# Strassen's products for pairs of q, k and v chunks in an attention and large-kernel convolution block

## The chip, the cores and the metric

The kernel runs on one core of a Trainium2 chip. The metric is the device time of one launch in microseconds (us); three runs of the kernel before gave 2863.83, 2867.12 and 2868.03 us, median 2867.12. A profiled execution is taken besides, and every reading of the trace is of that one.

The engines are named as in the profile: PE is TensorE (PEld its weight loads), DVE is VectorE, ACT is ScalarE, POOL is GpSimd, SP is SyncE, which here only issues DMAs. SBUF is the memory from which they work, PSUM the small memory into which TensorE writes its products.

## The reference

```python
x = x + attn(group_norm(x))            # x: 1 x 384 x 192 x 192, float32
x = x + convs(group_norm(x))
...
def attn(x):
    qkv = einsum('bchw,oc->bohw', x, w_qkv) + b_qkv      # 3*384 outputs, 384 inputs
    qkv = qkv.reshape(b, 3 * c, 96, 2, 96, 2).max(axis=(3, 5))
    qkv = depthwise_conv_3x3(qkv, w_dw) + b_dw
    q, k, v = split(qkv, 3, axis=1)                      # 8 heads of 48 channels
    q, k = q / norm(q), k / norm(k)                      # over the 9216 places
    attn = einsum('bhcn,bhdn->bhcd', q, k) * temperature
    out = sum(a_i * topk_softmax(attn, k_i) @ v)         # k_i = 24, 32, 36, 38
    return w_proj @ repeat_2x2(gelu(out)) + b_proj
...
def convs(x):   # seven depthwise convolutions of sizes 13 to 3, each with its own scale and shift, summed
```

Inputs, outputs and all arithmetic are float32.

## The kernel before

The 384 channels are three chunks of 128 partitions, so q, k and v together have nine output chunks, m = 0 to 8 (q: 0 to 2, k: 3 to 5, v: 6 to 8).

**Statistics (lines 289 to 585).** The whole of x is read once for the group statistics. Some q, k products of the first six blocks are made meanwhile: for the keys in `EARLY` (blocks 0 to 5, chunks 0 to 2, first sub-block) the two first input chunks are multiplied (line 429, `multiply`), ACT copies the half-made result to SBUF (`put_by`, line 440), and later back to PSUM (`fill`, line 269), where only the third input chunk is added.

**The stage that changes (lines 992 to 1051).** x is read again, twice, in 24 blocks of 8 rows, each of two sub-blocks of 4 rows (`sb`). The first pass (B = 0 to 23) makes q and k, the second (B = 24 to 47) v. A step is one output chunk of one sub-block: `project` (line 671) makes six products of 128x128 weights with 128x384 columns (three input chunks times two row pairs) into one PSUM tile of two banks; two such tiles take turns. `pool` (lines 683 and 690) takes the maximum over each 2x2 cell with one DVE reduction of 768 columns, and ACT adds the bias and writes 128x192 into the padded map `pool_t`. Once both sub-blocks of a chunk are there, `begin` (line 703, ACT) writes the centre tap of the depthwise 3x3 convolution, `taps` (line 719, DVE) adds the other eight, four to a step, each one instruction over 128x384, and `end` squares q and k for their norms (line 733) and moves the two last rows to the top of the padded map for the next block (line 738). After the last q, k chunk of a block, `turn` transposes the results in three pieces (TensorE line 748, ACT line 750) and `add_gram` adds them to the gram matrix (line 760). In the second pass the softmax of the gram matrix runs in small steps (`attend`, lines 797 to 945), one call a step.

The order on each engine is the order in which the program emits instructions, in this stage and in the one after: the list `late` (lines 949 to 952) says after how many steps each piece is emitted. Beside this, ACT normalizes x in place (line 651, six a block), POOL adds 2x2 cells of x for later (`sum_up`, lines 280 to 284), ACT and POOL spread the convolution's filters into DRAM (`strip`, lines 779 and 788), and SP's queue loads x two blocks deep (line 179).

**After it.** Attention times v (line 1131) needs, from its seventh block on, a copy that DVE makes of one head's rows (line 1102), behind two statistics of stored sums for each earlier block (line 1088). Then come the output projection (line 1459) and the large convolution (line 1371), which the change leaves alone.

## Time and profile before

| what | us |
|---|---|
| median of three runs | 2867.12 |
| the profiled execution | 2862.88 |
| its span | 2861.1 |
| PE busy, whole span | 2735.6 (96%) |
| DVE busy | 2498.5 (87%) |
| ACT busy | 1332.9 (47%) |
| POOL busy | 917.3 (32%) |
| first pass of the stage that changes | 166.3 to 1333.2 |
| second pass | 1333.2 to 1904.6 |
| attention times v, from its first product to the projection's | 1905.7 to 1960.8 |

The profile's slices cut the span in 40 equal parts of 71.5 us; a digit is the busy share in tenths. A group line gives line, engine, operation, the output and inputs by the program's names, the shape, the count, the busy time in us, the mean ns of one instruction, and the idle time of the engine just before the group's instructions with what ended it. Mean duration and rate differ: TensorE starts a product instruction every 0.323 us though one takes 486 ns from start to end. The granted TensorE clock was 0.995 of full speed.

### The profile page before, as it was taken

To read this page: it belongs to the slowest core of one execution; us is meant where nothing else is said; L and a number is where in the kernel's file an instruction comes from. 1 tells how busy PE (TensorE), PEld (TensorE's weight loads), DVE (VectorE), ACT (ScalarE), POOL (GpSimd) and SP (SyncE) were. 2 spreads that over 40 slices of the span, in tenths; PEclk is the share of its full clock that TensorE was granted. 3 is DMA by queue.
4 is the path that set the end of the run, shared out by engine and by line. 5 is a ranking of instruction groups with operands and counts; after the bars stand their busy time and mean duration, and the time that the engine had idled before them with its cause. 6 is when DMAs were issued, how large, how long until landed. Compare 5 with 4: busy or idle time off the path is not lost.

```text
span 2861.1 us, 37738 instructions
## 1 busy us (share of the span) xinstructions
PE 2735.6 (96%) x13662; PEld 1677.2 (59%) x13662; DVE 2498.5 (87%) x3484; ACT 1332.9 (47%) x2427; POOL 917.3 (32%) x1129
## 2 busy tenths in 40 slices
PE   0699999999999999999999999999999999999998
PEld 0356666666666666666655555545566666666666
DVE  6879998888878888788899998888789999999997
ACT  3755554444444444454444444444334444444443
POOL 4251231332323223241222222232114445444443
PEclk9899999999999999999999999999999999999999
DMA  9942432232422324232333333328889999999996
GB/s 389 419 151 65 134 114 87 81 126 72 135 74 92 111 70 137 67 126 81 100 108 107 108 109 116 115 69 234 234 206 282 270 275 275 256 271 271 270 275 168
DMA packets 269561, 475.75 MB, mean 166 GB/s; under 512 B 25858, under 2 KB 189968, under 8 KB 269248
## 3 DMA queue, kind: packets, MB, share of 16 engines
q1 hardware_dynamic: 204208, 301.51, 38.2%
q0 software_dynamic: 43328, 149.04, 15.5%
q10 hardware_dynamic: 21840, 22.81, 2.3%
q8 instruction: 108, 1.77, 0.3%
q14 instruction: 77, 0.63, 0.1%
HBM read 337.06 MB, written 136.20 MB: 165 GB/s over the span
## 4 chain that ended last, share of the span: by engine, by line
PE 85%; DVE 7%; DMA 5%; ACT 1%; issue 1%; POOL 0%; ACTq 0%; SPq 0%; DVEq 0%; POOLq 0%
PE qkv L671 51%; PE conv L1371 24%; PE pj L1459 4%; DVE v L719 3%; DMA xs<-in_x 3%; PE gram L760 2%; PE tr L748 2%; PE av L1131 1%; DVE mx L683 1%; PE qkv L429 1%; DVE acc L719 1%; DVE stats L535 1%; DMA v<-in_x 0%; DMA smj<-sums 0%; DMA wt<-zd 0%
## 5 line engine op out<-in xcount | busy, mean ns | idle before, releaser
L671 PE MATMUL qkv<-xt,wqk 128*128 128x384 f32 x3304 | 1082.5, 486 | 1.9 <-DVE mx L683 1.1
L671 PEld LDWEIGHTS qkv<-xt,wqk 128*128 128x128 f32 x3304 | 620.1, 190 | 417.1 <-DVE mx L683 4.5
L719 DVE SCALAR_TENSOR_TENSOR acc<-pooled,wd,acc 128x384 f32<-128x384 f32 (+2 forms) x1152 | 733.7, 637 | 30.6
L1371 PE MATMUL conv<-xp,wt 128*64 128x288 f32 (+1 forms) x6016 | 723.9, 404 | 2.4 <-issue 1.7
L690 ACT ACTIVATE pooled<-mx,bq 128x192 f32<-128x192 f32 x432 | 196.8, 456 | 900.2 <-DVE mx L683 898.1
L1371 PEld LDWEIGHTS conv<-xp,wt 128*64 128x64 f32 x6016 | 462.9, 137 | 260.8 <-issue 2.7
L683 DVE TENSOR_REDUCE mx<-qkv 128x192 f32<-128x768 f32 x432 | 412.3, 954 | 200.1 <-PE qkv L671 187.1
L671 PE MATMUL qkv<-xt,wv 128*128 128x384 f32 x1728 | 562.4, 487 | 2.5 <-DVE mx L683 2.2
L671 PEld LDWEIGHTS qkv<-xt,wv 128*128 128x128 f32 x1728 | 326.0, 190 | 233.4 <-DVE mx L683 9.8
L1351 DVE STREAM_TRANSPOSE xp<-xn 128x4608 f32<-128x4608 f32 (+1 forms) x107 | 445.4, 4163 | 18.0 <-PE conv L1371 10.6
L280 POOL TENSOR_TENSOR sum<-xt 128x192 f32<-128x192 f32 x128 | 87.9, 687 | 969.0 <-ACT xt L651 968.0
L719 DVE SCALAR_TENSOR_TENSOR v<-pooled,wd,v 128x384 f32<-128x384 f32 (+2 forms) x576 | 375.4, 652 | 15.2
L1379 ACT ACTIVATE co<-conv,cb 128x288 f32<-128x288 f32 x376 | 186.9, 497 | 386.1 <-PE conv L1371 381.3
L651 ACT ACTIVATE xt<-xt,gn 128x768 f32<-128x768 f32 x278 | 275.5, 1014 | 0.0
L1328 POOL TENSOR_TENSOR raw<-raw,up 128x2496 f32<-128x2496 f32 x46 | 230.0, 5001 | 38.2 <-DMA up<-pd 27.6
L1421 POOL DMA_DIRECT2D out<-o x194 | 107.4, 582 | 373.5 <-DVE o L1412 315.2
L1412 DVE STREAM_TRANSPOSE o<-co 128x2304 f32<-128x2304 f32 (+3 forms) x50 | 211.0, 4222 | 9.6 <-ACT co L1403 8.8
L1459 PE MATMUL pj<-v,wp 128*128 128x384 f32 x432 | 142.6, 489 | 1.0 <-ACT v L1138 0.7
L788 POOL DMA_DIRECT2D zd<-v x96 | 72.0, 756 | 216.1 <-ACT v L779 216.1
L1336 ACT ACTIVATE xn<-raw,par 128x2112 f32<-128x2112 f32 x48 | 103.1, 2148 | 25.4 <-POOL raw L1328 21.8
L1459 PEld LDWEIGHTS pj<-v,wp 128*128 128x128 f32 x432 | 80.9, 190 | 55.9 <-ACT v L1138 1.4
L281 POOL TENSOR_TENSOR sum<-sum,xt 128x192 f32<-128x192 f32 x128 | 100.9, 789 | 10.8
(296 smaller groups left out, 1914.6 us busy)
## 6 DMA issues: line engine op xcount, KB each, us to landing
xt<-in_x SPq DMA_DIRECT2D x96, 1152.0 KB, 7.4
raw<-in_x SPq DMA_DIRECT2D x182, 312.0 KB, 13.2
out<-o POOLq DMA_DIRECT2D x188, 288.0 KB, 8.4
wt<-zd SPq DMA_DIRECT2D x46, 1024.0 KB, 12.2
zd<-v POOLq DMA_DIRECT2D x96, 416.0 KB, 4.4
up<-pd SPq DMA_DIRECT2D x184, 156.0 KB, 12.6
xs<-in_x POOLq DMA_DIRECT2D x20, 768.0 KB, 10.7
smj<-sums SPq DMA_DIRECT2D x72, 192.0 KB, 3.0
```

The lines of the kernel that those rows point to most:

```text
L651: nc.scalar.activation(xt[:, j], xt[:, j], AF.Identity, bias=gn0[:, j, 1:2], scale=gn0[:, j, 0:1])
L671: nc.tensor.matmul(ps[:, r, : 2 * W], lhsT=wq[:, j, mm * P : (mm + 1) * P], rhs=xt[:, j, r * 2 * W : (r + 1) * 2 * W], start=(j == 0), sto ...
L683: nc.vector.tensor_reduce(mx, ps[:, :, : 2 * W].rearrange("p r (y w x) -> p r w y x", y=2, x=2), AX.XY, ALU.max,)
L690: nc.scalar.activation(pool_t[m][:, k : k + SR, 1 : 1 + WS], mx, AF.Identity, bias=bq[:, m : m + 1])
L719: nc.vector.scalar_tensor_tensor(acc[:, :nt], pool_t[m][:, k0 + dy : k0 + dy + nt, dx : dx + WS], wd[:, m, t : t + 1], acc[:, :nt], ALU.mu ...
L1328: eng.tensor_add(rv, rv, uv.unsqueeze(2).to_broadcast([P, (m1 - m0) * WS, 2]))
L1351: nc.vector.transpose(bass.AP(at.tensor, at.offset, [list(at.ap[0]), [NBQ, n], [1, NBQ], [NQ * NBQ, CC], [ME * NBQ, NE]],), bass.AP(row.te ...
L1371: nc.tensor.matmul(ps[h * MH : (h + 1) * MH, t0:t1], lhsT=wt[:, c, o : o + MH], rhs=d[:, c, g + 2 * t0 : g + 2 * t1 - 1 : 2, :], start=(e ...
L1379: nc.scalar.activation(co[:, c], ps, AF.Identity, bias=cb[:, cc : cc + 1])
L1412: nc.vector.transpose(bass.AP(at.tensor, at.offset, [list(at.ap[0]), [2 * W, n], [BC, NBQ], [W, 2], [1, BC]]), bass.AP(of.tensor, of.offse ...
L1421: engines[u % len(engines)].dma_start(out=bass.AP(out.tensor, out.offset + k * CC * HW + (2 * u + t0 * BR) * W, [[ME * UQ * W, CC * NE], [ ...
L1459: nc.tensor.matmul(ps, lhsT=wp[:, j, i * P : (i + 1) * P], rhs=v[:, j, b * RB : (b + 1) * RB, :].rearrange("p r w -> p (r w)"), start=(j = ...
```

## The change

**Seven products for eight.** Two output chunks form a pair: (3,4), (0,1), (2,5) and, for v, (6,7); chunk 8 stays single. The operands of Strassen's form are the pair's weights for input chunks 0 and 1, and the even and odd rows (y = 0, 1) of the sub-block in these chunks. `mix` forms four sums of weights (POOL, once for each pair), `differ` four differences of x for each sub-block (POOL, 128x384 each) and stores them in DRAM; the second pass reads them back (`differ_again`, SP's queue) and doesn't form them again. Input chunk 2 is multiplied as before. A product is now 128x128 with 128x384 columns of one row parity, that is two runs of 192 columns.

**Seeds.** Each PSUM bank is a tile of its own (six `banks`, where there were two tiles of two banks each). Partial sums that serve two results are copied from bank to bank by ACT (`seed`), and TensorE adds further products to both. A finished even-row result is copied to SBUF by ACT (`moved`), DVE takes the maximum with the odd-row result from PSUM (`larger`), one more DVE addition closes the second chunk of the pair, and `pool` takes the maximum of neighbours. The bias is no longer added here: it is folded into the convolution's bias (`shifted`), and the padding holds its negative (`pad`).

**Early results.** Half-made results are copied from and to PSUM in two instructions of 384 columns instead of one of 768 (`put_by`, `fill`); in the stage `put` takes the place of `fill`. The statistics' own small products use two of the six banks.

**Taps of v over two blocks.** `begin` and the taps of v run over 8 rows (768 columns) once in two blocks; block 0 (3 rows) and block 23 (5 rows) stay apart. `carry` copies the two border rows.

**Program order.** A unit (`pair`, `single` or `early_one`) has a head, a body and a tail. The loop emits the head of the next unit ahead of the tail of the one before, and inside them `act`, `tap`, `aside` and `other` emit at most so many waiting pieces for ACT, DVE, TensorE and POOL, first come first served but for priorities; a list of its own holds what waits on each engine. A single unit makes six products, an early one two. The transposes now use one PSUM tile, and their three pieces are emitted apart. Scratch space of the softmax lies in rows of v that aren't used yet.

The diff's core:

```diff
-    qkvps = ctx_a.enter_context(tc.tile_pool(name="qkvps", bufs=2, space=PSUM))
+    qkvps = ctx_a.enter_context(tc.tile_pool(name="qkvps", bufs=1, space=PSUM))
+    NBANK = 6
+    banks = [qkvps.tile([P, 512], F32, name=f"qkv{n}") for n in range(NBANK)]
+    ones = [0, 1]
+    def turnabout():
+        ones.append(ones.pop(0))
+        return [banks[SR * ones[-1] + r][:, : 2 * W] for r in range(SR)]
...
         if sb == 0 and (B, m) in begun:
-            ps = qkvps.tile([P, SR, 512], F32, tag="qkv", name="qkv")
-            nc.scalar.copy(ps[:, :, : 2 * W], halved(begun[B, m]))
+            ps = turnabout()
...
         def put_by(B, m, ps):
-            nc.scalar.copy(halved(begun[B, m]), ps[:, :, : 2 * W])
+            for r in range(SR):
+                nc.scalar.copy(halved(begun[B, m])[:, r], ps[r])
...
+        def mix(p, to=None):
+            s1, s2, s3, s4 = ((mixed[p] if to is None else to)[:, n] for n in range(4))
+            a11, a12, a21, a22 = (weights(m, k) for m in p for k in range(2))
+            yield nc.gpsimd.tensor_add(s1, a21, a22)
+            yield nc.gpsimd.tensor_sub(s2, s1, a11)
+            yield nc.gpsimd.tensor_sub(s3, a11, a21)
+            yield nc.gpsimd.tensor_sub(s4, a12, s2)
...
+        def rows_of(t):
+            return t.rearrange("p (r w) -> p r w", r=SR)
+        def part(B, sb, j, y):
+            return xts[B, sb][:, j].rearrange("p (r y w) -> p y r w", r=SR, y=2)[:, y]
...
+        def differ(B, sb):
+            t1, t2, t3, t4 = (rows_of(diffs(B, sb)[:, n]) for n in range(4))
+            b11, b12, b21, b22 = (part(B, sb, j, y) for j in range(2) for y in range(2))
+            for t, p, q in ((t1, b12, b11), (t3, b22, b12), (t2, b22, t1), (t4, b21, t2)):
+                yield nc.gpsimd.tensor_sub(t, p, q)
+            differed.add((B, sb))
+            nc.sync.dma_start(out=tds[2 * B + sb], in_=diffs(B, sb).rearrange("p q n -> p (q n)"))
+        differed = set()
...
+        def take(low=None):
+            fit = [n for n in idle if low is None or (n < NBANK // 2) == low]
+            n = (fit or idle)[0]
+            idle.remove(n)
+            return n
...
+        def product(n, w, xs, start=False):
+            assert start or n in used
+            used.add(n)
+            nc.tensor.matmul(
+                rows_of(cells[n]), lhsT=w, rhs=xs, start=start, stop=True, skip_group_check=True
             )
...
+        def seed(n, low=None):
+            k = take(low)
+            assert k in used
+            nc.scalar.copy(cells[k], cells[n])
+            return k
+        def moved(n, e):
+            nc.scalar.copy(e, cells[n])
+            idle.append(n)
+        def larger(e, n):
+            nc.vector.tensor_tensor(e, cells[n], e, ALU.max)
+            idle.append(n)
...
+        def pool(B, ms, sb, e):
...
+            t = t[:, :, k : k + SR, 1 : 1 + WS]
+            ev = e.rearrange("p (n w x) -> p n w x", n=len(ms) * SR, x=2)
+            t = t.rearrange("p n r w -> p n r w")
+            if len(ms) == 1:
+                nc.vector.tensor_tensor(t[:, 0], ev[:, :, :, 0], ev[:, :, :, 1], ALU.max)
+            else:
+                ev = e.rearrange("p (n r w x) -> p n r w x", n=len(ms), r=SR, x=2)
+                nc.vector.tensor_tensor(t, ev[..., 0], ev[..., 1], ALU.max)
+            if sb == 1 and (ms[0] < 2 * NJ or b % 2 == 0 or b == NB - 1):
+                for m in ms:
+                    acts.append((now + 1, 1, lambda m=m: begin(b, m), 1))
+                    if m >= 2 * NJ and b < NB - 1:
+                        acts.append((now + 5, 1, lambda m=m: carry(b, m), 0))
...
+        def pair(B, p, sb):
+            m1, m2 = p
+            n = {}
+            s1, s2, s3, s4 = (mixed[p][:, q] for q in range(4))
+            xs = [[part(B, sb, j, y) for y in range(2)] for j in range(NJ)]
+            t1, t2, t3, t4 = (rows_of(diffs(B, sb)[:, q]) for q in range(4))
+            def head():
+                n["a"] = take()
+                product(n["a"], weights(m1, 0), xs[0][0], True)
+                n["b"] = seed(n["a"], False)
+                act(2)
+                other(1)
+            def body():
+                e = n["ev"] = aw.tile([P, 2, 2 * W], F32, tag="e2", name="e2", bufs=2)
+                product(n["b"], s2, t2)
+                n["c"] = seed(n["b"])
+                act(1)
+                product(n["a"], weights(m1, 1), xs[1][0])
+                product(n["a"], weights(m1, 2), xs[2][0])
+                moved(n["a"], e[:, 0])
+                act(1)
+                other(1)
+                aside(1)
+                n["e"] = take()
+                product(n["e"], s3, t3, True)
+                product(n["b"], s1, t1)
+                n["d"] = seed(n["b"], True)
+                act(1)
+                aside(1)
+                product(n["c"], weights(m2, 1), t4)
+                product(n["c"], weights(m2, 2), xs[2][0])
+                moved(n["c"], e[:, 1])
+                act(1)
+                tap(6 if B <= NB else 3)
+                other(1)
+            def tail():
+                e = n["ev"]
+                product(n["d"], s4, xs[1][1])
+                product(n["d"], weights(m1, 2), xs[2][1])
+                tap(2 if B <= NB else 1)
+                larger(e[:, 0], n["d"])
+                product(n["b"], weights(m2, 2), xs[2][1])
+                tap(1 if B <= NB else 0)
+                larger(e[:, 1], n["b"])
+                nc.vector.tensor_tensor(e[:, 1], cells[n["e"]], e[:, 1], ALU.add)
+                idle.append(n["e"])
+                pool(B, p, sb, e.rearrange("p m n -> p (m n)"))
+                tap(0 if B <= NB else 1)
+                aside(1)
+            return head, body, tail
...
+        def put(B, m):
+            n = [take() for _ in range(2)]
+            assert used.issuperset(n)
+            t = begun[B, m].rearrange("p (r y w) -> p y r w", r=SR, y=2)
+            for y in range(2):
+                nc.scalar.copy(rows_of(cells[n[y]]), t[:, y])
+            put_back.append(n)
...
+        def first_of(q, width):
+            fit = [i for i, (when, w, f, *_) in enumerate(q) if when <= now and w <= width]
+            if fit:
+                return q.pop(min(fit, key=lambda i: q[i][3:]))
+        def act(n):
+            while n > 0:
+                got = first_of(acts, n)
+                if not got:
+                    return
+                n -= got[1]
+                got[2]()
...
+        def tap(n):
+            for _ in range(n):
+                got = first_of(taps_left, 1)
+                if got:
+                    got[2]()
...
+        def other(n):
+            for _ in range(n):
+                if others:
+                    others.pop(0)[1]()
...
+        def carry(b, m):
+            g = (b + 2) // 2
+            begun_v[m] = g
+            assert g < 3 or ended.get(m, -1) >= 2 * (g - 2)
+            k = R if b == 0 else 2 * R
+            nc.scalar.copy(pooled(b + 1, m)[:, 0:2, 1 : 1 + WS], pooled(b, m)[:, k : k + 2, 1 : 1 + WS])
+        accs, slots = {}, {}
...
         def begin(b, m):
             k0, n, na = rows(b)
             if m >= 2 * NJ:
                 o = b * R - 1 + k0
+                if b > 0:
+                    if b < NB - 1:
+                        o, n, na = o - R, 2 * R, 2 * R
+                    assert begun_v[m] == (b + 1) // 2
...
-                acc = a1.tile([P, R + 1, WS], F32, name=f"acc_{b}_{m}", tag="acc", bufs=8)
-            accs[b, m] = acc
+                k = (b * 2 * NJ + TURN.index(m)) % NA
...
+                slots[k] = b
...
+            for q, (r0, r1) in enumerate(((0, n), (n, na))):
+                if r0 == r1:
+                    continue
+                nc.scalar.activation(
+                    acc[:, r0:r1],
+                    pooled(b, m)[:, k0 + 1 + r0 : k0 + 1 + r1, 1 : 1 + WS],
+                    AF.Identity,
+                    bias=shifted[:, q, m : m + 1],
+                    scale=wd[:, m, 4:5],
+                )
+            for t in (0, 1, 2, 3, 5, 6, 7, 8):
+                taps_left.append((now + 1, 1, lambda t=t: tap_of(b, m, t)))
...
+        def units_of(B):
+            kv, q01, rest, vs = PAIRS
+            if B >= NB:
+                return [(pair, vs, 0), (single, 2 * NJ + 2, 0), (pair, vs, 1), (single, 2 * NJ + 2, 1)]
+            if (B, 0) not in begun:
+                return [(pair, p, sb) for p in (kv, q01, rest) for sb in range(2)]
+            first = [(pair, kv, 0), (early_one, 0, 0)]
+            if B == 0:
+                first = [(early_one, NJ, 0), (single, NJ + 1, 0), (early_one, 0, 0)]
+            return first + [
+                (pair, kv, 1), (early_one, 1, 0), (pair, q01, 1), (early_one, 2, 0), (single, NJ + 2, 0), (pair, rest, 1)
+            ]
+        units = [(B, u, *w) for B in range(2 * NB) for u, w in enumerate(units_of(B))]
...
+        def ready_next(B, n):
+            sb, j = (NORM if B < NB else NORM_V)[n]
+            normalize(B, sb, j)
+            ready.add((B, sb, j))
+            if B < NB and j == 1 and not (B < NEARLY and sb == 1):
+                queue(differ, 5, B, sb)
+            others.append((None, lambda: add_up(B, sb, j)))
+        ready = {(0, sb, j) for sb in range(2) for j in range(NJ)}
+        NEARLY = EARLY[-1][0] + 1
...
+        def hook(B, u, n_units):
+            if u == 0 and 1 <= B < 2 * NB - 1:
+                for i in range(2):
+                    load(B + 1, i)
+            if B < NB:
+                when = {n_units - 4: (0, 1), n_units - 3: (2,), n_units - 2: (3,), n_units - 1: (4, 5)}.get(u, ())
+                ahead = [(B + 1, n) for n in when]
+            else:
+                ahead = [(B + 1, n) for n in {2: (0, 1), 3: (2,)}.get(u, ())]
+                ahead += [(B, n) for n in {0: (3, 4), 1: (5,)}.get(u, ())]
+            if B == NB - 1:
+                ahead = [(B + 1, n) for n in {2: (0, 1), 3: (2,)}.get(u, ())]
+            for c, n in reversed(ahead):
...
+            before = None
...
+                assert kind is not pair or (B, sb) in differed, (B, u)
+                head, body, tail = kind(B, what, sb)
+                head()
                 if attention:
                     next(attention[0], None)
...
-                            at(s + 1, add_up, B + 1, *divmod(n, NJ))
-                if sb == 1:
-                    at(s + 1, begin, b, m)
-                    for h in range(2):
-                        at(s + 2 + h, taps, b, m, h)
-                    at(s + 4, end, b, m)
-                    if m == 2 * NJ - 1:
-                        for i in range(chunks(b)):
-                            at(s + 4 + i, turn_next, b, i)
-                            at(s + 5 + i, gram_next)
-                        if b == NB - 1:
-                            at(s + 5 + i, begin_attention)
-            for s in sorted(late):
-                for f, args in late[s]:
-                    f(*args)
+                if before:
+                    before()
+                hook(B, u, len(units_of(B)))
+                body()
+                if attention and kind is pair and (B < NB + 2 or B % 2):
+                    next(attention[0], None)
+                if now + 1 < len(units):
+                    n = units[now + 1]
+                    if n[2] is early_one and not put_back:
+                        put(n[0], n[3])
```

## The prediction

> **What bounds the kernel now.** I read first the slices and the chain of waits, then the groups by shape, then the chain in order of time inside the stage that changes. The slices and the chain:
>
> ```profile
> PE   0699999999999999999999999999999999999998
> DVE  6879998888878888788899998888789999999997
> ACT  3755554444444444454444444444334444444443
> ...
> PE qkv L671 51%; PE conv L1371 24%; PE pj L1459 4%; DVE v L719 3%; DMA xs<-in_x 3%; PE gram L760 2%; PE tr L748 2%; PE av L1131 1%; DVE mx L683 1%; PE qkv L429 1%; DVE acc L719 1%; DVE stats L535 1%; DMA v<-in_x 0%; DMA smj<-sums 0%; DMA wt<-zd 0%
> ```
>
> TensorE is full from the third slice on, and half of the span is line 671, the products of q, k and v. DVE is the second engine, at 80 to 90% there. The groups by shape (columns: count, then busy us and mean ns of one, then idle before):
>
> ```profile
> L671 PE MATMUL qkv<-xt,wqk 128*128 128x384 f32 x3304 | 1082.5, 486 | 1.9 <-DVE mx L683 1.1
> L671 PE MATMUL qkv<-xt,wv 128*128 128x384 f32 x1728 | 562.4, 487 | 2.5 <-DVE mx L683 2.2
> L719 DVE SCALAR_TENSOR_TENSOR acc<-pooled,wd,acc 128x384 f32<-128x384 f32 x1074 | 684.1, 637 | 28.6
> L683 DVE TENSOR_REDUCE mx<-qkv 128x192 f32<-128x768 f32 x432 | 412.3, 954 | 200.1 <-PE qkv L671 187.1
> ```
>
> A float32 product is two instructions: 3304 and 1728 are 1652 and 864 products. The chain in order of time shows one block of the first pass (start, length, what):
>
> ```profile
> 453.06 34.86 PE qkv L671 x108
> 487.92 0.66 PE tr L748 x6
> 488.57 3.87 PE qkv L671 x12
> 492.45 0.68 PE gram L760 x8
> ...
> 503.53 34.86 PE qkv L671 x108
> ```
>
> It repeats after 50.47 us. 34.86/108 gives 0.3228 us for an instruction, so 0.6455 for a product; 72 products are 46.5, three transposes with grams 4.0. Nothing is left over: here TensorE's issue alone is the bound. Busy time of an early block (its products half made before) and of this one, by PE, PEld, DVE, ACT, POOL:
>
> ```profile
> core 0: us, PE busy (x) PEld busy (x) DVE busy (x) ACT busy (x) POOL busy (x), PEclk, DMA share, GB/s
> 317.14:361.15 44.01, 42.98 (x164) 26.61 (x163) 40.49 (x61) 25.42 (x53) 10.17 (x13) 1.00 0.34 109
> 453.06:503.53 50.47, 50.47 (x187) 31.26 (x187) 40.95 (x61) 23.43 (x50) 13.93 (x20) 1.00 0.27 89
> ```
>
> In the early block DVE has the same work in 44.0 us, and TensorE already loses 1.0.
>
> [...] The trace shows products in program order. [...] the trace's one such row, line 864 (PSUM and SBUF in, 96x384), took 544, and I use that. [...] taps average 682 ns at 520 to 530 us, with GpSimd adding, and 616 at 530 to 542, with it idle.
>
> **The products.** A pair with one sub-block takes 11 products where it took 12 (7 for 8 over two input chunks, 4 for the third). An ordinary first-pass block falls from 72 to 66, an early one from 60 to 56, block 0 from 56 to 53, a v block from 36 to 34. The sum is 1188+280+53+816 = 2337 against 2516: 179 fewer, 179 x 0.6455 = **115.5 us**, the most that the idea itself can give. Row-parity operands are two runs of 192 columns; I take their rate as unchanged.
>
> **Ordinary block, first pass (18).** TensorE: 66 x 0.6455 + 4.0 = 46.6. DVE: 48 taps stay. In the trace four stand in 2.57 us, 0.635 each with GpSimd's share: 30.5. The 12 reductions (0.88 from start to start) go. Each of 6 pair units brings two maxima from PSUM, an addition and a pooled maximum at 0.544; where the next does not read the result, neighbours overlap by 0.08 as reductions and taps do, so some 2.0 a unit, 12.0 a block (13.1 without overlap). With 8 us more of GpSimd differences at 8% disturbance (0.6) and, in some blocks, the variance steps, 43 to 44.5: 92 to 95% of TensorE's time. ACT: 23.4 now, less 12 biases at 0.456, plus 30 PSUM copies. Their nearest row is line 750, 384 columns at 0.477: 14.3. Together 32 of 47. Per unit the DVE and ACT work fits, but with less slack than before, so I add 0.4 for hand-offs: **47.0**, that is 18 x 3.47 = **62 us gained**. Bounds 46.6 and 48.4.
>
> **The added waits.** Each pair has three seeds, copied by ACT from bank to bank between products. Between the product that makes a seed and the one that needs it stand three products, 1.94 us (two transposes' groups more at times). A hand-off needs about 0.16 (486 less 323, the product's tail) and 0.48: ACT may be 1.3 late. In front of a seed on ACT can stand a normalization (1.01), a first tap (0.70) or the filter strip (1.75, once a block); I take no stall on the mean. If a seed is late, all TensorE work queues behind it, and DVE's maxima behind that. Banks: the next unit needs banks that DVE's maxima free; the first is wanted again some 2.6 us (four products) after it is finished, the slack DVE may lag by.
>
> **Early blocks (5).** DVE: 30.5 + 4 pairs x 2.0 + 4 single units x 0.82 (a PSUM maximum and a 192-column one at 0.35) = 41.8; TensorE 36.1+4.0 = 40.2. So DVE becomes the bound: 42.6 taken for 44.0, **7 us gained** (0 to 17). Block 0: nothing.
>
> **Second pass (24 blocks).** It took 571.4 (1333.2 to 1904.6), 557.7 of it products. Now 816 x 0.6455 = 526.7, and the rest stays (last transposes, attention, waits): **31 us gained**. DVE has 12 taps of 768 columns a block, 0.637 + 384 x 1.04 ns = 1.04 each by the slope between reductions and additions, so 12.5, with 4.0 for pairs and 1.6 for singles: 18.1 of 22. Single waits when its queue is full: 26 to 36.
>
> **End of the stage.** Taps of v over two blocks come late. By the limits written into the units, about 13 of the last 24 double taps fit in the last block; 11 x 1.04 and 24 five-row taps at 0.755 remain after the last product: 29 us. Today DVE ends its taps at 1915.7, 11 after it. The attention-times-v stage needs DVE for its seventh block (head copy), which starts 19 us after the last product; now at 29+5 statistics = 35. Then 18 blocks at TensorE's pace of 1.93 take 35 where they took 38: **12 us lost** (0 to 18).
>
> **Start.** Fills and stores around line 429 become two copies of 0.477 for one of 0.79, some 60 times, 10 us of ACT work partly beside DVE's statistics; GpSimd's 12 small mixes and 8 differences (about 1.0 us each; 192 columns take 0.5 to 0.7) stand ahead of its waiting sums, but 10 products cover the first. Against it 9 memsets (4.8) go. **2 lost** (0 to 8). Differences go to DRAM on SP's queue, in pass one behind the next loads of x: 1.5 MB a block where the DMA engines are 27 to 34% busy, and in pass two are read back 14 us before use, where a load of 1152 KB lands in 7.4. Nothing.
>
> **Sum**: 62+7+31-12-2 = 86. The profiled execution took 2862.9 for a span of 2861.1, and lies 4.2 below the median of the runs, 2867.1. So 2777 in its terms, **2781** in those of the median.
>
> **Rivals.**
> A. DVE becomes the bound in pass one. For: early blocks lose 1.0 at 92% DVE. Against: their load is uneven, the new units are alike. Without overlap and with disturbance DVE has 44.6; held to 92% this is 48.4 a block: 18 x 2.07 = 37 gained, early blocks at 46.7 lose 13, pass two gains 30, end and start lose 14: 40 gained, 2827.
> B. Slower: one seed in each pair comes late. There are 179 pair units; my gain is 86/179 = 0.48 us each. From that mean stall on the kernel is slower. Two long ACT jobs ahead of one seed would give about 0.75: 134 lost against 86, 2915. Against it: ACT is at 68%, and 1.3 us of slack.
> C. Better: TensorE issues without gaps, early blocks reach 41, the end is hidden: 70+15+36 = 121, 2746. It exceeds 115 only since today's waits go too.
>
> **Chances.** Forecast 0.66 (2755 to 2808), A 0.17, B 0.07, C 0.10. The range 2748 to 2828 takes in the forecast, most of A and half of C. Within 0.2% (about what a measurement can tell from no change) 0.02, which I take from the tail between A and B; faster 0.91, slower 0.07.
>
> **What would show it.** Ordinary blocks 47.0 apart; a first-pass DVE busy above 43; idle time of TensorE before seeded products near nothing (B: half a us a unit, released by ACT); early blocks 42 to 43 with TensorE waiting on DVE; v blocks 22 apart; a head copy waiting behind taps after the stage. The prediction fails if a row-parity product takes longer than 0.6455, or if ACT's order exposes seeds.

## The result and the profile after

The changed kernel takes 2912.47 us (median of four runs, 2907.49 to 2914.58), the kernel before beside it 2867.57 (2863.83 to 2870.82): a ratio of 1.0154, 95% interval 1.0135 to 1.0174. It is slower by 45 us where 86 us less were forecast. Its profiled execution took 2914.29 us, with a span of 2912.5.

The stage boundaries, read from the first and last products of the two profiles, say where (v's first product starts at 1333.6 in the kernel before; 1333.2 is its weight load):

| part | before | after | change | predicted |
|---|---|---|---|---|
| up to the first product of the stage | 166.3 | 165.2 | -1.1 | +2 |
| first pass (q and k) | 1167.3 | 1210.8 | +43.5 | -69 |
| second pass (v) | 571.0 | 549.8 | -21.2 | -31 |
| last product to the first product of the projection | 56.2 | 82.5 | +26.3 | +12 |
| from there to the end | 900.3 | 904.2 | +3.9 | 0 |

The slices of the page and its chain by line, as shown for the kernel before:

```profile
PE   0689889999999999999999999959999999999998
DVE  6879998999999989999688988887889999999997
ACT  3756565665666656666565555535334444444443
...
PE qkv L773 32%; PE conv L1809 24%; DVE v L1057 15%; PE pj L1897 4%; DVE e L789 3%; DMA xs<-in_x 2%; PE av L1569 2%; PE gram L1121 2%; DVE pooled L841 1%; DVE e L896 1%; PE tr L1100 1%; PE qkv L457 1%; DVE stats L564 1%; ACT xt L705 0%; DVE pooled L838 0%
```

The products had 51% of the chain and the taps (line 719, now 1057) 3% and 1% in two groups; now they have 32% and 15%. The groups by shape say what grew:

```profile
L1057 DVE SCALAR_TENSOR_TENSOR v<-pooled,wd,v 128x384 f32<-128x384 f32 x1077 | 797.1, 749 | 23.5
...
L773 PE MATMUL qkv<-xt,wqk 128*128 128x384 f32 x1732 | 630.5, 489 | 6.8 <-DVE e L789 6.8
...
L773 PE MATMUL qkv<-xt,wv 128*128 128x384 f32 x1152 | 397.2, 486 | 0.0
```

A product with its operand in x takes what it took (486 to 489 ns). **The tap does not: the same instruction on the same 384 columns has gone from 637 to 749 ns.** Busy time of an early block and of an ordinary one (before: 44.01 and 50.47 us long, DVE 40.49 and 40.95 busy, POOL 10.17 and 13.93):

```profile
core 0: us, PE busy (x) PEld busy (x) DVE busy (x) ACT busy (x) POOL busy (x), PEclk, DMA share, GB/s
317.00:366.00 49.00, 43.04 (x165) 25.65 (x164) 47.03 (x74) 32.16 (x70) 19.18 (x21) 1.00 0.41 131
862.93:914.33 51.40, 47.40 (x176) 28.58 (x175) 47.80 (x73) 31.61 (x68) 25.68 (x29) 1.00 0.38 127
```

The ordinary block was forecast at 47.0 and is 51.4 long. TensorE is busy for 47.4 of it, about its 46.6 of work, and VectorE for 47.8 where 43 to 44.5 were forecast. Neither is full. The timeline of the same block shows why (start, length, what; xN is a run of N instructions). VectorE:

```profile
869.75 5.07 DVE L1057 SCALAR_TENSOR_TENSOR v<-pooled,wd,v 128x384 f32<-128x384 f32 x8
...
885.94 8.23 DVE L1057 SCALAR_TENSOR_TENSOR v<-pooled,wd,v 128x384 f32<-128x384 f32 x8
894.57 1.50 DVE L1057 SCALAR_TENSOR_TENSOR v<-pooled,wd,v 128x384 f32<-128x384 f32 x1
```

GpSimd:

```profile
886.00 2.69 POOL L748 TENSOR_TENSOR v<-xt 128x384 f32<-128x384 f32 x2 [15.39 <-ACT xt L705]
888.65 2.58 POOL L748 TENSOR_TENSOR v<-xt,v 128x384 f32<-128x384 f32 x2
...
894.64 1.01 POOL L748 TENSOR_TENSOR v<-xt 128x384 f32<-128x384 f32 x1
```

Eight taps take 5.07 us while GpSimd ends an issue of DMAs and then stands, and 8.23 while it forms four differences and then a cell sum (three additions). The single tap at 894.57 takes 1.50 instead of 0.61 beside one difference. The chain of what ended last goes the same way in this block:

```profile
871.39 3.90 PE qkv L773 x12
...
879.93 3.27 PE qkv L773 x10
...
886.59 1.25 DVE v L1057
887.87 1.25 DVE v L1057
889.14 1.25 DVE v L1057
...
894.70 6.09 PE qkv L773 x18
```

It is TensorE's up to 883, then VectorE's as long as the differences last, then TensorE's again. So the block isn't held by an average load: two bursts of differences, at 886 and at 902, each put VectorE on the chain.

### The profile page after: what moved, and what is told of

It is laid out like the page before. It is cut to its first block, busy times and chain, and to the rows that moved or that the text cites. A ratio compares the mean times of both kernels' runs of the same rounds, so it can differ in the third digit from the quotient of the medians.

```text
span 2912.5 us, 38866 instructions
## 1 busy us (share of the span) xinstructions
PE 2657.4 (91%) x13304; PEld 1608.2 (55%) x13304; DVE 2615.9 (90%) x3689; ACT 1559.8 (54%) x2968; POOL 1164.6 (40%) x1332
## 4 chain that ended last, share of the span: by engine, by line
PE 66%; DVE 24%; DMA 4%; issue 4%; ACT 2%; POOL 1%; DVEq 0%; ACTq 0%; POOLq 0%
PE qkv L773 32%; PE conv L1809 24%; DVE v L1057 15%; PE pj L1897 4%; DVE e L789 3%; DMA xs<-in_x 2%; PE av L1569 2%; PE gram L1121 2%; DVE pooled L841 1%; DVE e L896 1%; PE tr L1100 1%; PE qkv L457 1%; DVE stats L564 1%; ACT xt L705 0%; DVE pooled L838 0%
## 5 line engine op out<-in xcount | busy, mean ns | idle before, releaser
L1057 DVE SCALAR_TENSOR_TENSOR v<-pooled,wd,v 128x384 f32<-128x384 f32 (+3 forms) x1368 | 1064.7, 786 | 30.9 <-POOL pooled L728 1.0
L773 PE MATMUL qkv<-xt,wqk 128*128 128x384 f32 x1732 | 630.5, 489 | 6.8 <-DVE e L789 6.8
L773 PEld LDWEIGHTS qkv<-xt,wqk 128*128 128x128 f32 x1732 | 330.0, 191 | 236.9 <-DVE e L789 9.2
L780 ACT COPY qkv<-qkv 128x384 f32<-128x384 f32 x537 | 251.4, 468 | 295.0 <-PE qkv L773 216.5
L773 PE MATMUL qkv<-xt,wv 128*128 128x384 f32 x1152 | 397.2, 486 | 0.0
L785 ACT COPY e<-qkv 128x384 f32<-128x384 f32 x432 | 204.6, 474 | 338.5 <-PE qkv L773 338.0
L789 DVE TENSOR_TENSOR e<-qkv,e 128x384 f32<-128x384 f32 x432 | 234.6, 549 | 125.5 <-PE qkv L773 76.3
L773 PEld LDWEIGHTS qkv<-xt,wv 128*128 128x128 f32 x1152 | 218.0, 190 | 149.7
L773 PE MATMUL qkv<-diff,v 128*128 128x384 f32 x468 | 184.3, 503 | 52.3 <-DVE e L789 44.1
L773 PE MATMUL qkv<-v 128*128 128x384 f32 x372 | 144.2, 497 | 43.0 <-DVE e L789 36.8
```

Of the source, the lines that this page charges most:

```text
L773: nc.tensor.matmul(rows_of(cells[n]), lhsT=w, rhs=xs, start=start, stop=True, skip_group_check=True)
L780: nc.scalar.copy(cells[k], cells[n])
L785: nc.scalar.copy(e, cells[n])
L789: nc.vector.tensor_tensor(e, cells[n], e, ALU.max)
L1057: nc.vector.scalar_tensor_tensor(acc[:, :nt], pooled(b, m)[:, k0 + dy : k0 + dy + nt, dx : dx + WS], wd[:, m, t : t + 1], acc[:, :nt], ALU ...
```

## The experiments

In all of them "first pass" runs from 165 us to the first v product and "second pass" from there to the start of the last one (1211.0 and 549.3 us in the changed kernel, 1168.6 and 570.5 in the one before; some tenths of a us beside the table, whose boundaries are each kernel's own), and taps are those of 384 columns from 500 to 1300 us. Theory 1, later called the contention theory, is that GpSimd's differences slow the taps (rival A's mechanism, larger). Against it stood rival B's, that the pairs' own seeds and hand-offs cost the time (theory 2, later the theory of the pairs' chains), and ACT's added work.

**Fewer or more differences.** Two kernels and their edits:

```diff
-                yield nc.gpsimd.tensor_sub(t, p, q)
+                n = SR if B < 6 else 1
+                k = W if B < 6 else 8
+                yield nc.gpsimd.tensor_sub(t[:, :n, :k], p[:, :n, :k], q[:, :n, :k])
```

> From block 6 of the first pass on, the four differences of a sub-block cover 8 columns of one row instead of 384 (the products then use stale differences: that part of the computation is left out); instructions, waits and transfers stay. Theory 1 (GpSimd's additions slow DVE's taps, and DVE bounds the first pass): taps in ordinary blocks fall from about 750 to 670 ns, DVE's busy time from 47.8 to 43.8 us a block, the block from 51.4 to about 47.3, total 2912 - 18 x 4.1 = 2838 (2825 to 2855); the early blocks, which keep their differences, stay at about 50. Theory 2 (seeds late on ACT): ACT has the same work, so 2905 to 2915. Theory 3 (DVE's own number of operations and its hand-offs bound the block, GpSimd has no part): 2900 to 2915.

```diff
+                if B >= 6:
+                    nc.gpsimd.tensor_sub(t, p, q)
                 yield nc.gpsimd.tensor_sub(t, p, q)
```

> From block 6 on each difference is formed twice, with the same result: GpSimd's work on differences doubles, nothing else changes. Theory 1: each us of GpSimd addition costs DVE 0.4 us, so 9.5 us more a block cost about 3.9, blocks at 55, total 2912 + 70 = 2982 (2960 to 3000), taps near 830 ns. Theories 2 and 3: 2905 to 2920, unless differences come too late for their products, which would show as TensorE waiting on GpSimd.

Measured: 2829.05 us with narrow differences (ratio to before 0.9875, 0.9857 to 0.9893) and 2999.37 with doubled ones (1.0483, 1.0446 to 1.052), 83 less and 87 more than the changed kernel, both within the ranges of theory 1. The taps of the first, then of the second:

```profile
L1059 DVE SCALAR_TENSOR_TENSOR v<-pooled,wd,v 128x384 f32<-128x384 f32 x798 | 522.5, 664 | 17.2
```

```profile
L1059 DVE SCALAR_TENSOR_TENSOR v<-pooled,wd,v 128x384 f32<-128x384 f32 x677 | 561.5, 838 | 14.4
```

664, 749, 838 ns for none, one and two sets of differences. TensorE's waits for VectorE between 500 and 1300 us go the same way (total, times, longest), in the changed kernel, then with narrow and with doubled differences:

```profile
PE qkv L773 <- DVE e L789: 61.7, 30, 2.6
PE qkv L775 <- DVE e L791: 1.6, 5, 0.4
PE qkv L775 <- DVE e L791: 107.7, 36, 3.6
```

All products, seeds and copies were as before in number, and with narrow differences TensorE was busy for 795.9 of 800 us between 500 and 1300. The first pass took 1127 us there. This shows that the differences cost 84 us and that the pairs without them do what was forecast. That products wait for differences which come late is not the reason: in the whole stage of the changed kernel TensorE and its weight loads wait 1.4 us for them.

Not all of the 84 us need be the taps themselves. The trace of the changed kernel has stretches of 3.4 us in which TensorE's granted clock is half (0.5 in the trace's record of the clock; 27 us of the first pass in all). Of 16 ordinary blocks, measured from gram to gram, three have one; they take 53.4 us, the other 13 take 51.5. With narrow differences no ordinary block has such a stretch. That is some 6 us of the 84, an estimate (3 x 1.9). Whether TensorE's standing brings the stretches on, no run tests.

**Less work for ACT.** Squares of one row, normalization of half the columns, from block 6 on:

```diff
-                junk[:, :na], accs[b, m][0][:, :na], AF.Square, accum_out=ssq[:, m, b : b + 1]
+                junk[:, : 1 if b >= 6 else na], accs[b, m][0][:, : 1 if b >= 6 else na], AF.Square, ...
-            nc.scalar.activation(xt[:, j], xt[:, j], AF.Identity, ...)
+            k = SR * W if 6 <= B < NB else 2 * SR * W
+            nc.scalar.activation(xt[:, j, :k], xt[:, j, :k], AF.Identity, ...)
```

> ACT is relieved from block 6 to the end of the first pass: the squares for the norms cover one row of four and the normalizations half of the columns (both parts of the computation are left out), some 4 us less ACT work a block. Theory 1: DVE waits for ACT copies about 1.6 us a block today, a part of it goes: 2890 to 2912. Theory 2: ACT's lateness is the stall, most of 18 x 4 us is won: 2845 to 2870. Theory 3: 2890 to 2912.

Measured: 2935.53 us (1.0249, 1.0227 to 1.0272), 23 slower than the changed kernel, which no theory expected. ACT was the less busy by 52 us between 500 and 1300, and the time rose: ACT was not the limit. The taps took 775 ns instead of 749. 26 ns on 48 taps of 18 blocks are 22 us, as much as the whole loss. Laying the starts and ends of all taps beside those of GpSimd's additions in the two traces, a tap has 182 ns of differences running beside it here and 146 in the changed kernel: the differences, whose start ACT's normalizations set, fall more on taps and less on other VectorE work. That reading fits in size, but nothing was run on it alone, and the traces hold a rival that fits better. Busy times between 500 and 1300 us in the changed kernel, then in this one (the last three figures are granted clock, DMA share and GB/s):

```profile
500.00:1300.00 800.00, 738.29 (x2698) 445.73 (x2697) 738.03 (x1140) 487.35 (x1038) 380.63 (x439) 0.99 0.37 125
500.00:1300.00 800.00, 737.11 (x2616) 445.91 (x2615) 730.37 (x1112) 435.23 (x1009) 378.46 (x431) 0.96 0.36 122
```

TensorE is busy as long in both, but with 82 instructions fewer: its clock is 0.96 for 0.99. The stretches at half clock fill 85 us of the first pass, for 27 in the changed kernel. The two ordinary blocks without any take 51.9 us, against 51.5 in the changed kernel; eight with 3.4 us of them take 52.9 and six with 6.8 take 54.4. So the slower taps alone go with about 0.4 us a block and the clock with most of the loss. Why the stretches became more frequent stays open.

**A copy in place of the difference.** From block 6 on:

```diff
-                yield nc.gpsimd.tensor_sub(t, p, q)
+                if B >= 6:
+                    yield nc.gpsimd.tensor_copy(t, p)
+                else:
+                    yield nc.gpsimd.tensor_sub(t, p, q)
```

> The changed kernel with each difference of the blocks from the sixth on replaced by a GpSimd copy of its first operand, 384 columns wide as before; the subtraction is left out, so that the pairs work on other data. [...] a copy has one input and slows a tap less, 2835 to 2860, taps 660 to 690. Theory that any GpSimd instruction of this width does it in proportion to its time: copies of 0.57 us for 32 rows of the head stage point to about 0.6 us each, half of an addition: 2865 to 2880, taps about 705.

Measured: 2835.05 us (0.9885, 0.987 to 0.99). GpSimd's copies, then the taps:

```profile
L749 POOL COPY diff<-xt 128x384 f32<-128x384 f32 x64 | 43.8, 711 | 175.6 <-ACT xt L705 175.4
```

```profile
L1060 DVE SCALAR_TENSOR_TENSOR v<-pooled,wd,v 128x384 f32<-128x384 f32 x794 | 530.6, 677 | 17.1
```

The first expectation holds: 677 ns is within 660 to 690. A copy of the same width takes 0.71 us on the mean (0.51 with no tap beside it), longer than the 0.6 that the second one set, and yet nearly all of the loss is gone: the taps are 13 ns slower than with narrow differences (664), where the differences made them 85 slower (749). What hurts most is not that GpSimd works, but that it reads two inputs, and longer: a us of a copy beside a tap costs it 0.21 us, a us of a difference 0.57.

**Plain products in the first pass.** Two kernels. In the first the differences are still formed there, for the second pass alone; in the second they are formed in the second pass:

```diff
-                return [(pair, p, sb) for p in (kv, q01, rest) for sb in range(2)]
+                return [(single, m, sb) for p in (kv, q01, rest) for m in p for sb in range(2)]
...
+            return [x for k, m, sb in us for x in ([(single, c, sb) for c in m] if k is pair else [(k, m, sb)])]
```

> The changed kernel with the first pass computed by plain products, 12 of them a block, no pairs; GpSimd still forms the differences there and stores them for the second pass, which keeps its pairs. Contention theory: the taps are still slow (about 740 ns each) because of the differences, VectorE has 47 to 48 us of work in a block, but TensorE now needs 50.5, so that most of this is covered: 50.5 to 51.5 a block, early blocks 45 to 47, 2880 (2868 to 2900). Theory of the pairs' chains (seeds, and handing over between units, are what costs): taps at about 640 ns once no pairs run, and 50.5 a block and 44 in early ones: 2866 or less.

> As the run with a plain first pass, but the differences are formed by GpSimd in the second pass, just ahead of the products that read them, and not stored or loaded (those of block 0 apart). Contention theory: taps of the first pass return to 635 to 645 ns, the first pass to 1167 us; in the second pass VectorE has 38.6 us of work in a block of 45.8 and gains 3.5 of contention, which TensorE's work covers for the most part: 2872 (2862 to 2890). If the second pass is as sensitive as the first was, it loses 20 and the time is 2890. Theory of the pairs' chains: as the other run, 2866, the taps alike in both.

Measured: 2888.94 us (1.0081, 1.0055 to 1.0107) and 2930.77 us (1.0222, 1.0194 to 1.0249), the first within the contention theory's range, the second outside all. The first of them between 500 and 1300 us, its busy times and two of its groups:

```profile
500.00:1300.00 800.00, 800.00 (x2949) 492.14 (x2948) 734.05 (x1169) 374.05 (x776) 389.07 (x456) 1.00 0.37 126
```

```profile
L1057 DVE SCALAR_TENSOR_TENSOR v<-pooled,wd,v 128x384 f32<-128x384 f32 x760 | 574.4, 765 | 16.3
L789 DVE TENSOR_TENSOR e<-qkv,e 128x384 f32<-128x384 f32 x190 | 104.4, 550 | 43.2 <-PE qkv L773 43.0
```

There are no pairs here, and the taps are as slow as with them: 765 ns. But TensorE is busy for all of the 800 us. The same disturbance costs nothing in an ordinary block whose products need 50.5 us. Its first pass took 1183.5 us, 15 more than before, and that lies in the early blocks, where TensorE has less to do. In the other kernel the first pass took 1162.5 and the taps 642 ns, as the contention theory has it; since TensorE is full in the ordinary blocks of both, the 21 us between the two are what the differences cost plain early blocks. My expectation for its second pass, and so for its total, was wrong: it took 614.5 us instead of 549.3. I had set 3.5 us of contention against a block of 45.8, but 549.3 / 24 is 22.9, and 45.8 is two blocks. Eight differences a block bring VectorE from 19.3 to about 23 of these 22.9 us, so by this price no room is left:

```profile
1400.00:1850.00 450.00, 408.68 (x1217) 230.88 (x1216) 399.17 (x544) 225.31 (x380) 298.22 (x282) 0.97 0.27 97
```

TensorE, full for 494 of 500 us in the changed kernel's second pass, is busy for 409 of 450, and the taps of 768 columns took 1308 ns for 1071. But VectorE is busy for only 399 of the 450. TensorE's products wait 40.5 us there for seeds, while the seeds wait 53.8 for VectorE's maxima, which free the banks; the weight loads wait 57 for nothing that the trace names; and the clock of 0.97 in this line takes up to 14. That the contention is what costs is in part argued here: the differences are made just ahead of the products that read them, and no run separates slow taps from late differences.

**Early blocks without pairs.** Plain products and no differences for the six blocks up to the last early one, in both passes; the ordinary ones as changed:

```diff
+        def formed(B, sb):
+            return EARLY[-1][0] < B
...
-            if B < NB and j == 1 and not (B < NEARLY and sb == 1):
+            if B < NB and j == 1 and formed(B, sb) and not (B < NEARLY and sb == 1):
```

> The changed kernel with plain products in the six blocks up to the last early one, in both passes, and no differences formed for them; pairs in both halves of the 18 ordinary blocks. Contention theory: early blocks return from 49 or 50 to 44 or 45 us, 27 saved, and the second pass loses 6 times 0.9: 2890 (2882 to 2899). Theory that the early blocks are held by the order of their units and not by VectorE: 2908 to 2920.

Measured: 2893.86 us (1.0093, 1.0074 to 1.0112). The first pass is 26 us shorter (1184.9), the second 6 longer (555.2), both as expected. As this kernel took away the pairs and the differences of these blocks together, it doesn't tell them apart by itself; the 21 us of the two kernels with plain products do.

**The end of the stage.** In the changed kernel TensorE stands for 29 us after six products of attention times v. TensorE, then GpSimd, then VectorE:

```profile
1928.66 1.50 PE L1569 MATMUL av<-v,bd 128*32 128x384 f32 x6 [2.86 <-DVE e L789]
1959.42 0.85 PE L1569 MATMUL av<-hx,bd 96*32 96x384 f32 x1 [29.27 <-POOL hx L1542]
```

```profile
1958.34 3.81 POOL L1542 COPY hx<-v 32x384 f32<-32x384 f32 x7 [40.01 <-DVE t L1548]
```

```profile
1928.82 12.48 DVE L1057 SCALAR_TENSOR_TENSOR v<-pooled,wd,v 128x768 f32<-128x768 f32 x12
1941.22 11.30 DVE L1057 SCALAR_TENSOR_TENSOR v<-wqk,wd,v 128x480 f32<-128x480 f32 x16
1952.44 5.69 DVE L1057 SCALAR_TENSOR_TENSOR v<-pooled,wd,v 128x480 f32<-128x480 f32 x8
```

The first head copies (`hx`), whose rows of v were long ready, start when the last tap ends. I took this for memory: the copy's tile lies where the stage's tiles lay. The first attempt exchanged two pools, so that `hx` comes to lie lower, and let GpSimd make more of the copies:

```diff
-            tc.tile_pool(name="bx", bufs=3) as bx,
             tc.tile_pool(name="b1", bufs=1) as b1,
+            tc.tile_pool(name="bx", bufs=3) as bx,
...
-                    elif c == 1 and b >= NBB // 4:
+                    elif c == 1 and b >= 14:
```

> After the stage the tiles of the head copies are placed ahead of those of the stored sums, so that they no longer lie over the padded maps which the last taps read, and GpSimd makes the middle head's copies up to block 13 where DVE took over at block 6. If the 29 us wait of attention times v is for memory that the late taps still read (theory of the end), TensorE goes on at once: 20 to 33 us less, 2880 to 2892. If it waits for the rows of v that the taps write, or for the queue of taps itself: within 5 us of 2912.

Measured: 2910.5 us (1.0154, 1.0139 to 1.0169), no gain; TensorE still waits 29.3 us. I take it that the place lower down was still within the tiles that the stage gives back together; the trace doesn't show places. The second attempt took it to the other side of the memory, where the blocks of x had been:

```diff
-            tc.tile_pool(name="bx", bufs=3) as bx,
-            tc.tile_pool(name="b1", bufs=1) as b1,
+            tc.tile_pool(name="bx", bufs=3, side="right") as bx,
+            tc.tile_pool(name="b1", bufs=1, side="right") as b1,
...
-                    elif c == 1 and b >= NBB // 4:
+                    elif c == 1 and b >= 24:
```

> The changed kernel with the tiles for the gathered heads and for the input sums taken from the memory of the input blocks, on the other side, which the taps never touch, and with GpSimd making the middle head copies of all 24 blocks in place of VectorE after the sixth. Theory A (memory): in the changed kernel the first head copy waits 40 us for the last tap because its memory was given back by the pool that the taps read; with other memory TensorE begins the head stage right behind the last product at about 1929 instead of 1959, the taps run beside it to 1958, and VectorE's 47 statistics of the sums (24 us) then end last, at about 1985 instead of 2008: 2889 (2880 to 2897). Theory B (the rows themselves are late): the stage needs the last rows of v in any case, and nothing is regained: 2906 to 2914.

Measured: 2910.98 us (1.0149, 1.012 to 1.0179). The cause of the wait is confirmed (the attempt before had GpSimd's copies up to block 13, and kept the wait), the gain is not: attention times v begins at 1927.2 and the projection's products at 1984.2, 24 us sooner, and then TensorE stands again:

```profile
DVE stats_s L1526 <- DMA sm<-sums: 19.8, 18, 6.6
PEld pj L1897 <- DVE cell L1913: 19.7, 2, 19.4
```

The projection's first results wait for VectorE's line 1913, which stands behind its 47 statistics of the stored sums, and these behind the last tap and behind their loads. VectorE gets there at 2008.3, within 3 us of the changed kernel. The third attempt gives the loads ten tiles in place of three (`bufs=10`):

> The changed kernel with the end of the stage mended as before (memory of the head tiles, middle head copies on GpSimd) and with ten tiles for the input sums in place of three. In the earlier run TensorE began the projection 24 us sooner and then stood 19 us for VectorE, whose statistics of the sums came after the last tap at 1962 and waited 20 us for their loads. Theory A: the loads now stand ready, VectorE needs 24 us for 47 statistics behind the last tap, and the projection goes on at about 1988 in place of 2008: 2893 (2886 to 2900). Theory B: the loads are bound by the DMA engines themselves (9.4 MB at some 200 GB/s take 47 us), and little is won: 2903 to 2911.

Measured: 2901.18 us (1.0122, 1.0102 to 1.0141), between the two expectations: some 10 us regained. Theory B's 200 GB/s is near what the DMA engines moved in the changed kernel (213 GB/s from 1959 to 2009 us); here they moved 315 to 392 in the slices from 1972 to 1996. VectorE reaches line 1913 at 2001.1 and still waits 10.9 us for loads:

```profile
1957.01 6.77 DVE L1057 SCALAR_TENSOR_TENSOR v<-pooled,wd,v 128x480 f32<-128x480 f32 x8
1963.82 1.94 DVE L1526 BATCH_NORM_STATS2 stats_s<-sm 128x6 f32<-128x384 f32 x4
1972.58 3.08 DVE L1526 BATCH_NORM_STATS2 stats_s<-sm 128x6 f32<-128x384 f32 x6 [6.82 <-DMA sm<-sums]
```

So three things are late there, one behind the other: the head copies, the statistics' loads, and VectorE itself, with 24 us of statistics behind the last tap.

**A version that beats both.** Pairs only in the first half of each of the 18 ordinary blocks, plain products elsewhere; a first form of it, with the memory and the head copies of the second attempt and three tiles for the sums, formed the second halves' differences in the second pass:

```diff
-                return [(pair, p, sb) for p in (kv, q01, rest) for sb in range(2)]
+                return [x for p in (kv, q01, rest) for x in [(pair, p, 0)] + [(single, m, 1) for m in p]]
```

> A version meant to be faster than both: pairs only in the first half of each ordinary block of the first pass, plain products in the second half and in the five early blocks; the differences of the first halves are formed in the first pass, the others in the second pass; and the memory and the head copies of the run on the end of the stage. Contention theory: TensorE needs 48.6 us a block, VectorE 43.0 and 0.41 of 4.2, about 45; taken 49 for 51.4, 41 saved on 18 blocks, 27 on the early ones, 24 at the end: 2822 (2808 to 2845). Theory of the pairs' chains: each pair costs what it did, half of the loss stays, and the end alone is regained: 2860 to 2870.

Measured: 2859.85 us (0.9975, 0.9967 to 0.9984). As a total that is the other theory's figure and misses the contention theory's range. The parts say otherwise: the first pass is 1131.5 us, 37 less than in the kernel before (165 to 1333.6, 1168.6) and more than the contention theory asked for; the second is 578.9, as in the kernel above that formed differences in the second pass, which this expectation had not reckoned with. The second form has no differences for the second halves at all, plain products for them in the second pass, and ten tiles for the sums:

> A version meant to be faster than both. In the first pass pairs only for the first half of the 18 ordinary blocks, plain products elsewhere, the differences formed for these first halves alone and used again in the second pass, where the other halves have plain products; the head tiles and the tiles of the input sums in the memory of the input blocks, ten of the latter in place of three, and all middle head copies on GpSimd. Contention theory: the first pass as in the half version, 1132 us (34 less than before); the second pass saves 18 times 0.45 of the 571 of before; the end of the stage 62 for 56; the rest 3 more: 2832 (2822 to 2845). If differences were not what costs, the first pass would gain no more than in the half version and the second pass would stay at 579: 2850 or more.

Measured: **2821.04 us (0.9838, 0.9821 to 0.9855), faster than both**, 45 us less than the kernel before and 91 less than the changed one, and 1 us below the expected range. Its busy times in the first and the second pass:

```profile
500.00:1300.00 800.00, 798.23 (x2955) 489.24 (x2954) 725.15 (x1210) 447.79 (x948) 316.81 (x388) 1.00 0.37 116
1310.00:1850.00 540.00, 538.63 (x1730) 319.88 (x1729) 434.60 (x702) 264.94 (x429) 155.76 (x192) 1.00 0.41 132
```

TensorE is full in both. VectorE has 725 of 800 us, and as only half of the differences are there, its taps take 697 ns. In the profiled executions the first pass gives 35 us of the gain and the second 12; the end of the stage takes what it took before (57 us for 56), and from the projection on it takes 6.5 us longer, which stays open. With plain early blocks throughout, the first pass took 1162.5 us without pairs, 1131.5 with pairs in the first halves and 1184.9 with pairs in both halves of the ordinary blocks.

## Why the prediction was wrong

**The step that failed** is in "Ordinary block": "With 8 us more of GpSimd differences at 8% disturbance (0.6)". The 8% came from taps that averaged 682 ns at 520 to 530 us against 616. Two errors are in it. In that window GpSimd was adding for less than half of the time, so that a mean over it is not the price of an overlap. And what it added there were cell sums of 192 outputs, not differences of 384. Fitting each tap's time to what ran beside it (500 to 1300 us of the changed kernel) gives 614 ns free, 0.57 us more for each us of a difference and 0.31 for each us of a sum; in the kernel before a sum costs 0.20. A tap that lies wholly within differences takes 1238 ns, twice its time. The eight differences of a block take 9.4 us (8 x 1.18), not 8 x 1.0, and 75% of the differences' time falls on taps: 749 - 637 ns on 48 taps are 5.4 us a block, where 0.6 were forecast. By the fit some 4.0 of them are the differences' own (0.57 x 146 ns x 48) and the rest is the sums, which fall on taps more often than before. Neither of the two failures that the prediction named came about: the rate of a product stayed, and between 500 and 1300 us no product of the changed kernel waits for a seed.

- **Products**: right. 179 fewer, at the same rate: the longest unbroken run of the changed kernel, 674 instructions from 1705.18 us on, takes 217.41 us, 0.3226 each for 0.3228 before. So row-parity operands cost nothing that shows; with narrow differences TensorE is 99% busy.
- **Ordinary block**: -62 forecast. 17 us longer in fact (18 x 0.93). It follows from the failed term, and from a second one: 0.4 for hand-offs. With VectorE at 47.8 the block took 51.4, since the differences come in bursts and the taps have fixed places between products, so VectorE can't use the slack between bursts. That the bursts are the reason is read from the chain; no run spread them out. With narrow differences the blocks take 47.2, for 47.0 forecast.
- **Early blocks**: -7 forecast for all five, 5 or 6 us longer each in fact (49 and 50 for 44). The run without pairs there gained 26 in the first pass. If the two gains add up, narrow differences and plain early blocks together would take 84 + 26 from 1210.8: 1101 against 1098 forecast. So in sum the rest of the first pass was right; whether pairs without differences would have gained the 7 in the early blocks, no run shows.
- **Second pass**: -31 forecast, -21.2 measured. The tap of 768 columns took the forecast 1.04 us in the run of 12 at 1928.82 us (12.48 us), with GpSimd idle. TensorE waits 5.2 us for seeds in front of products and some of the 16.3 us in front of weight loads, which I had put at nothing, and 3 us are transposes and grams of the last block that now fall into it (84 instructions for 56).
- **Seeds**: no bound in pass one, as forecast. In the stage products wait 19.6 us (24 times) for ACT's seeds and 87.7 for VectorE's maxima, weight loads 35.7 and 115.2. The products' waits are idle time of TensorE: none of the products behind a waiting one ran in it.
- **End of the stage**: 12 forecast, 26 measured. The taps end 32 us after the last product (29 forecast). But I let the wait begin at the seventh block's copy, and all copies wait, from block 0 on, since their memory is given back with the taps' maps. The stage began 1 us after the last product before; with the first copy put behind the taps, the forecast's own 29 us would have made it some 28 later, not 12 (an estimate).
- **Start**: 2 lost forecast, 1 gained. The 3.9 us of the rest stay open.

**The rivals.** B named 2915 and the time is 2912, but that is luck, since its mechanism is refuted: products wait 19.6 us for seeds in all and weight loads at most 35.7 more, not 134, and relieving ACT did not help. C needed TensorE without gaps, and it stood 61.7 us for VectorE between 500 and 1300 alone. A had the mechanism, VectorE as the bound in pass one, but at 48.4 and 46.7 us a block, since it used the same 8%; VectorE's measured 47.8, held to A's 92%, gives 52.0 for the 51.4 that were measured.

In the burst taps of 1.25 us stand beside differences of 1.3 us, one to one: such a pair takes less than the 1.6 us of the two alone (0.61 and 1.0), one after the other, and a tap twice what it takes alone. A us of a sum beside a tap costs it 0.31 us and a us of a copy 0.21, against 0.57 for a difference. By what means GpSimd and VectorE hold each other up, no run shows.

## What to carry to other kernels

A disturbance is priced by laying single instructions beside single instructions of the disturber, of the same kind as the one to be added, not by a mean over a window that it fills in part. Ask whether VectorE has room for what it loses to work given to GpSimd: here the same differences cost 0 under a block of 50.5 us and 4 to 5 us under one of 46.6, and in the first pass half of the saving with half of the differences was worth more than all of it. When one wait at the end of a stage is taken away, list what VectorE has still to do behind it before counting the gain.

## What the runs showed of the hardware

- A VectorE instruction with two SBUF inputs (the tap, 384 columns) takes 614 to 619 ns alone and 1238 within GpSimd two-input additions of 384 columns in the changed kernel (means of 1183 to 1293 over the runs), which themselves take 1.0 us with no tap beside them and 1.2 with one (1.3 in the burst). Within narrow additions of 8 columns it takes 655, within GpSimd copies of 384 columns 778.
- The VectorE maximum with one input from PSUM (384 columns) takes 551, 549 and 550 ns with no, one and two sets of differences, while the pooled maximum, of two SBUF inputs, goes from 563 to 666 and 660.
- A GpSimd copy of 384 columns on 128 partitions takes 0.51 us with no tap beside it and 0.74 with one, a difference 1.0 and 1.2.
- In the first pass the granted TensorE clock fell to half, in stretches of 3.4 or 6.8 us, for 27 us in the changed kernel, 75 with doubled differences and 85 with less work for ACT, where TensorE often stood for VectorE; for 0 to 3.4 us in the kernel before, with plain products, with copies and with half of the pairs, where it was full or nearly so. No run tests which brings on the other.
